# Matrix shapes, TensorE's order and the placing of side work in a graph layer followed by masked attention

## The chip, the cores and the metric

The kernel runs on one core of a Trainium2 chip. TensorE (PE in the profile) multiplies matrices into PSUM, VectorE (DVE), ScalarE (ACT) and GpSimd (POOL) work on SBUF, the first two also on PSUM, and all DMAs of this kernel are issued from SyncE's queue (SP). The metric is the device time of one launch in microseconds (us); lower is better. All data are float32, except for the mask, which is held as bytes.

## The reference

x is (8, 2048, 256), adj is (2048, 2048), sparse with a full diagonal. Two layers follow each other, both with a residual and a layernorm:

```python
# layer 0
A_norm = A + eye(n)
deg = A_norm.sum(0) + A_norm.sum(1) - diagonal(A_norm)
A_hat = A_norm * rsqrt(deg)[:, None] * rsqrt(deg)[None, :]
agg = einsum('nm,bmd->bnd', A_hat, x)
h = relu(batchnorm(agg.reshape(-1, d) @ W1.T + b1))     # 256 -> 512
x = layernorm(x + batchnorm(h @ W2.T + b2))             # 512 -> 256
# layer 1: 4 heads of 64
q, k, v = split(x @ W)
scores = einsum('bhid,bhjd->bhij', q, k) / 8 + where(adj == 0, -inf, 0)
x = layernorm(x + einsum('bhij,bhjd->bhid', softmax(scores), v))
```

## The kernel before

**Layer 0.** The adjacency is transposed on PE and kept in SBUF. For each of the 8 batch entries and each chunk of 512 nodes (32 chunks) PE aggregates (L209) and multiplies by W1 (L235); the hidden rows go to DRAM as h_d, and DVE writes the mask, one byte for an element, to mask_d in 16 pieces. Once the statistics of the first batchnorm are complete, a second loop (L280 to L304) loads h again, applies batchnorm and ReLU on ACT (L287), multiplies by W2 (L295), adds the bias and takes statistics on DVE and stores y_d. In its iteration i == 4, SP's queue also gets the load of the projection weights wq and of the whole mask (16 x 2048 bytes in each of 128 partitions).

**Layer 1, `attention`.** The work is cut into 64 units: batch entry b, head pair hp (two heads of 64 columns) and a chunk k of 512 queries, in that order of nesting. A unit has eight steps of two key tiles each (GJ = 2, key tile = 128 keys). All units and steps are numbered through, step g = unit * 8 + step. In each step

- `scores` computes, key tile by key tile, keys by queries for both heads into a PSUM tile ps_s of two banks; here each of the four 64 x 64 quarters of the array takes one head and one half of the 128 keys (L449). DVE subtracts the mask from it into an SBUF tile pt (L459), ACT takes the exponential (L465; a factor of 2^40 makes a masked element zero), and POOL adds the pt tiles up in two halves for the sum of the softmax (L470, L472);
- `weigh`, two steps behind (LAG = 2), multiplies pt with V into ps_o; the four quarters are two heads by two halves of the keys (L484), so that ps_o has two banks, whose halves `finish_copy` adds (ACT L494, DVE L495).

Side work hangs on the steps: `project` makes one of q, k, v for a chunk of 512 rows (L414, L423, copied by ACT); `prep_load`, `prep_bn`, `prep_res`, `prep_norm` and `prep_t` load a chunk of y and x of the next batch entry, apply the second batchnorm, turn y by PE transposes (L379), add the residual, layernorm, store x1 and turn it for the projections (L397); for a unit that has ended, `finish_sums` sums acc over the partitions (L505), and `finish` turns sums and output (L516, L527), divides and adds the residual; `emit`, in units of the second head pair, does the last layernorm and stores the rows. A layernorm is a chain DVE, POOL (the power of -1/2, L345), DVE, ACT.

A step has two slots for side work: slot 0 between scores and weigh, slot 1 after weigh. The 24 projections of a batch entry are spread one to a step. The PSUM pools are ps_s with 2 tiles of two banks, ps_o with 1 tile of two banks and ps_m with 2 tiles of one bank, which projections, transposes and sums share. All four chunks of the first batch entry are prepared in the written order before the first scores; the order in which an engine runs its instructions is otherwise set by the framework, which lists for each engine what it takes to be ready, earlier written first.

Of the kernel before, what the change touches and what calls it, by code (L numbers as in the profile page):

```python
# [28 lines left out]
def tile_gcn_then_masked_attention(  # L29
# [64 lines left out]
    with ExitStack() as kept:  # L94
# [182 lines left out]
        with tc.tile_pool(name="l0b", bufs=3) as lp, tc.tile_pool(  # L277
            name="psy", bufs=4, space=PSUM
        ) as psy:
            for i in range(NALL):  # L280
                h = hp_.tile([P, NH, CH], F32, name="h")
                nc.sync.dma_start(h, h_d[i])
                if i == 4:
                    nc.sync.dma_start(wq, wqkv.rearrange("(c p) f -> p c f", p=P))
                    nc.sync.dma_start(mask, mask_d)
                for f in range(NH):
                    nc.scalar.activation(  # L287
                        h[:, f, :], h[:, f, :], AF.Relu,
                        bias=sh1[:, f : f + 1], scale=sc1[:, f : f + 1],
                    )  # L290
                y = lp.tile([P, NO, CH], F32, name="y")
                for o in range(NO):
                    py = psy.tile([P, CH], F32, name="py")
                    for f in range(NH):
                        nc.tensor.matmul(  # L295
                            py,
                            w2s[:, f, o * P : (o + 1) * P],
                            h[:, f, :],
                            start=(f == 0),
                            stop=(f == NH - 1),  # L300
                        )
                    nc.vector.tensor_scalar(y[:, o, :], py, b2s[:, o : o + 1], None, op0=ALU.add)
                    nc.vector.bn_stats(st2[:, o, i, :], y[:, o, :])
                nc.sync.dma_start(y_d[i], y)  # L304
# [5 lines left out]
def attention(tc, x, out, adj, mask, wq, ident, ones, mhalf, sc2, sh2, sall, y_d, x1_d):  # L310
# [16 lines left out]
    with ExitStack() as ctx:  # L327
        ap_ = ctx.enter_context(tc.tile_pool(name="attn", bufs=2))
        ps_s = ctx.enter_context(tc.tile_pool(name="ps_s", bufs=2, space=PSUM))
        ps_o = ctx.enter_context(tc.tile_pool(name="ps_o", bufs=1, space=PSUM))  # L330
# [27 lines left out]
        def prep_load(b, k):  # L358
            yt[b, k] = ap_.tile([P, NO, CH], F32, name="yt")
# [77 lines left out]
        def scores(u, g):  # L437
# [4 lines left out]
            for j in range(g * GJ, (g + 1) * GJ):  # L442
                ps = ps_s.tile([P, 2, CH], F32, name="ps_s")

                for q in range(2):
                    for h in range(2):
                        hs = slice(h * HD, (h + 1) * HD)
                        c0 = j * P + q * HD
                        nc.tensor.matmul(  # L449
                            ps[q * HD : (q + 1) * HD, h, :],  # L450
                            kt[hs, c0 : c0 + HD],
                            qt[hs, k * CH : (k + 1) * CH],
                            start=True,
                            stop=True,
                        )
                pss.append(ps)
# [17 lines left out]
        def weigh(u, g):  # L474
            b, hp, _ = units[u]
            if g == 0:
                outs[u] = ps_o.tile([P, 2, CH], F32, name="ps_o")
            for j in range(g * GJ, (g + 1) * GJ):
                pt = probs.pop((u, j))

                for h in range(2):
                    for q in range(2):
                        qs = slice(q * HD, (q + 1) * HD)
                        nc.tensor.matmul(  # L484
                            outs[u][h * HD : (h + 1) * HD, q, :],
                            qkv[b, hp][2][qs, j, h * HD : (h + 1) * HD],
                            pt[qs, h, :],
                            start=(j == 0),
                            stop=(j == NT - 1),
                        )  # L490

        def finish_copy(u):
            ot = ap_.tile([P, CH], F32, name="ot")
            nc.scalar.copy(ot, outs[u][:, 0, :])  # L494
            nc.vector.tensor_add(ot, outs[u][:, 1, :], ot)  # L495
# [44 lines left out]

        per_b = HP * NCH * NG
        side = {}

        def at_step(g, s, f, *args):
            side.setdefault((g, s), []).append((f, args))

        def prep_at(b, k, g):
            at_step(g - 6, 0, prep_load, b, k)
            at_step(g - 2, 1, prep_bn, b, k)
            at_step(g, 0, prep_res, b, k, 0)  # L550
            at_step(g, 1, prep_res, b, k, 1)
            at_step(g, 1, prep_norm, b, k)
            for d in range(ND):
                at_step(g + 4, d, prep_t, b, k, d)

        for b in range(B):
            g0 = b * per_b
            for c in range(NCH):
                for w in range(3):
                    at_step(g0 + 3 + 3 * c + w, 1, project, b, 1, c, w)  # L560
            if b + 1 < B:
                for k, g in enumerate((17, 23, 29, 48)):
                    prep_at(b + 1, k, g0 + g)
                for c, g in enumerate((35, 41, 47, 54)):
                    for w in range(3):
                        at_step(g0 + g + 2 * w, 1, project, b + 1, 0, c, w)
        for u in range(len(units)):
            g0 = (u + 1) * NG
            at_step(g0 + 1, 1, finish_copy, u)
            at_step(g0 + 4, 0, finish_sums, u)  # L570
            at_step(g0 + 5, 0, finish, u)
            at_step(g0 + 5, 1, emit, u)

        for k in range(NCH):
            prep_load(0, k)
# [3 lines left out]
            prep_norm(0, k)  # L579
            for d in range(ND):  # L580
                prep_t(0, k, d)
            for w in range(3):
                project(0, 0, k, w)

        total = len(units) * NG
        LAG = 2
        for g in range(total + NG):
            if g < total:
                scores(*divmod(g, NG))
            for f, args in side.get((g, 0), ()):  # L590
                f(*args)
            if 0 <= g - LAG < total:
                weigh(*divmod(g - LAG, NG))
            for f, args in side.get((g, 1), ()):
# [210 lines left out]
```

## Time and profile before

| | |
|---|---|
| time, median of 3 runs | 4069.35 us (4067.44 to 4070.09) |
| profiled execution: its time | 4070.09 us |
| profiled execution: span | 4068.3 us |
| granted TensorE clock, mean | 0.979 |
| last matmul of the second loop of layer 0 (L295) ends | about 1415 us |
| first scores (L449) | 1443.3 us |
| DVE L459, mask subtraction | x1024, 1219 ns each |
| ACT L465, exponential | x1024, 1055 ns each |
| POOL L472 and L470, sums | x768 and x128, 2365 ns each |
| PE L414 (q, k) and L423 (v) | 256.1 and 130.9 us busy |
| PE L505 (sums) | 69.2 us busy |
| PE L379, L397, L516, L527 (transposes) | 42.7, 45.1, 41.7, 39.6 us busy |

A float32 matmul is shown as two instructions (two passes). The form "64*64" in a row is the part of the array that one instruction uses, rows by columns. Matmuls are pipelined, so a row's mean duration (606 ns for L449) is longer than the distance from one wave to the next, and the time that a group takes is read from start to start.

### The profile page before, as it was taken

Reading aid. Unit: us, or ns where it says so; the run is one execution under the profiler, and the core shown is the slowest. Engines: PE = TensorE matmul, PEld = TensorE weight load, DVE = VectorE, ACT = ScalarE, POOL = GpSimd, SP = SyncE. Lnnn points to the kernel's source line nnn. Section 1 sums busy time; section 2 is a strip of 40 time slices with the busy share of each in tenths; the row PEclk is TensorE's granted clock in tenths of the full one; section 3 lists DMA queues with packets and bytes.
Section 4 is the critical chain, followed back from the end, with each engine's and each line's share of the span. In section 5 each row is a group of like instructions: output and inputs, shape, how many; then the busy total and the mean of one; then the engine's idle time right before and its main releaser. Section 6 shows DMA issues by size and latency. Waiting matters only on the chain. (4 is left out here: it accounts for less than half of the span.)

```text
span 4068.3 us, 54545 instructions
## 1 busy us (share of the span) xinstructions
PE 3855.4 (95%) x22818; PEld 1544.6 (38%) x22818; DVE 1883.5 (46%) x2589; ACT 1667.1 (41%) x2077; POOL 2288.4 (56%) x1083
## 2 busy tenths in 40 slices
PE   7999999999989989999999999999999999999986
PEld 5444444444434433333333333333333333333322
DVE  5211111111124435666665665665656666566565
ACT  5000000000024345555555555555555555555544
POOL 0011101110100038888878987988888888888897
PEclk8999999999999989999999999999999999999998
DMA  5111101110146620000010000000000000000000
GB/s 215 65 47 52 52 27 46 52 52 31 47 158 219 208 80 22 22 32 27 17 42 22 22 32 22 32 32 22 32 22 32 27 27 27 27 17 17 6 6 17
DMA packets 94491, 198.34 MB, mean 49 GB/s; under 512 B 7072, under 2 KB 73120, under 8 KB 83872
## 3 DMA queue, kind: packets, MB, share of 16 engines
q1 hardware_dynamic: 94240, 194.80, 13.8%
q8 instruction: 181, 2.97, 0.3%
q14 instruction: 70, 0.57, 0.0%
HBM read 106.70 MB, written 88.08 MB: 48 GB/s over the span
## 5 line engine op out<-in xcount | busy, mean ns | idle before, releaser
L472 POOL TENSOR_TENSOR acc<-acc,pt 128x1024 f32<-128x1024 f32 x768 | 1816.2, 2365 | 320.8 <-ACT pt L465 272.9
L459 DVE TENSOR_TENSOR pt<-ps_s,mask 128x1024 f32<-128x1024 f32 x1024 | 1208.6, 1219 | 791.7 <-PE ps_s L449 765.2
L465 ACT ACTIVATE pt<-pt 128x1024 f32<-128x1024 f32 x1024 | 1069.4, 1055 | 769.7 <-DVE pt L459 743.5
L449 PE MATMUL ps_s<-qt,kt 64*64 64x512 f32 x8192 | 1021.8, 606 | 81.2 <-DVE pt L459 79.5
L484 PE MATMUL ps_o<-pt,v 64*64 64x512 f32 x8192 | 1009.6, 600 | 41.4 <-DVE ot L495 41.4
L209 PE MATMUL pa<-at,xb 128*128 128x512 f32 x2048 | 886.9, 593 | 0.0
L187 POOL TENSOR_SCALAR xb<-xb,dinv 128x256 f32<-128x256 f32 x112 | 103.0, 943 | 865.3 <-DMA xb<-in_x_dram 853.3
L209 PEld LDWEIGHTS pa<-at,xb 128*128 128x128 f32 x2048 | 389.5, 190 | 488.1 <-issue 483.0
L449 PEld LDWEIGHTS ps_s<-qt,kt 64*64 64x64 f32 x8192 | 287.1, 134 | 655.4 <-issue 427.9
L484 PEld LDWEIGHTS ps_o<-pt,v 64*64 64x64 f32 x8192 | 299.5, 134 | 613.3 <-issue 506.8
L242 ACT ACTIVATE h<-ph,b1s 128x512 f32<-128x512 f32 x128 | 87.9, 687 | 993.9 <-PE ph L235 993.9
L228 DVE TENSOR_TENSOR ag<-pa,dbc 128x512 f32<-128x512 f32 x64 | 44.3, 692 | 771.2 <-PE pa L209 771.2
L470 POOL TENSOR_TENSOR acc<-pt 128x1024 f32<-128x1024 f32 x128 | 302.9, 2366 | 83.3 <-ACT pt L465 83.3
L414 PE MATMUL pm<-x1t,wq 128*128 128x512 f32 x512 | 256.1, 625 | 0.5 <-ACT x1t L398 0.5
L295 PE MATMUL py<-h,w2s 128*128 128x512 f32 x512 | 224.7, 602 | 13.7 <-ACT h L287 13.7
L235 PE MATMUL ph<-ag,w1s 128*128 128x512 f32 x512 | 225.1, 592 | 0.0
L350 ACT ACTIVATE x<-x,ln_nm,ln_rs 128x256 f32<-128x256 f32 x256 | 134.1, 589 | 208.7 <-DVE ln_nm L346 208.7
L88 POOL TENSOR_TENSOR rs<-rs,mhalf 128x4 f32<-128x4 f32 (+1 forms) x2 | 1.7, 870 | 379.9 <-DVE rs L87 379.9
L243 DVE BATCH_NORM_STATS2 st<-h 128x6 f32<-128x512 f32 x128 | 88.9, 694 | 148.5 <-ACT h L242 148.5
L295 PEld LDWEIGHTS py<-h,w2s 128*128 128x128 f32 x512 | 98.8, 194 | 139.5 <-issue 116.5
L414 PEld LDWEIGHTS pm<-x1t,wq 128*128 128x128 f32 x512 | 88.4, 192 | 166.5 <-issue 125.2
L287 ACT ACTIVATE h<-h,sh,sc 128x512 f32<-128x512 f32 x128 | 93.3, 801 | 132.5 <-DMA h<-h_d 122.9
(79 smaller groups left out, 1800.7 us busy)
## 6 DMA issues: line engine op xcount, KB each, us to landing
h_d<-h SPq DMA_DIRECT2D x32, 1024.0 KB, 3.9
h<-h_d SPq DMA_DIRECT2D x32, 1024.0 KB, 5.9
a<-in_adj_dram SPq DMA_DIRECT2D x16, 1024.0 KB, 8.3
xb<-in_x_dram SPq DMA_DIRECT2D x32, 512.0 KB, 3.9
y_d<-y SPq DMA_DIRECT2D x32, 512.0 KB, 6.3
yt<-y_d SPq DMA_DIRECT2D x32, 512.0 KB, 3.3
x<-in_x_dram SPq DMA_DIRECT2D x32, 512.0 KB, 3.8
x_d<-x SPq DMA_DIRECT2D x32, 512.0 KB, 2.8
```

Source lines behind the costliest of these rows:

```text
L187: nc.gpsimd.tensor_scalar(t4[:, j, :], t4[:, j, :], dv, None, op0=ALU.mult)
L209: nc.tensor.matmul(pa, xs[b][m // TPC][:, m % TPC, d * P : (d + 1) * P], at[:, m, c * CH : (c + 1) * CH], start=(m == 0), stop=(m == NT - 1),)
L235: nc.tensor.matmul(ph, w1s[:, d, f * P : (f + 1) * P], ag[:, d, :], start=(d == 0), stop=(d == ND - 1),)
L295: nc.tensor.matmul(py, w2s[:, f, o * P : (o + 1) * P], h[:, f, :], start=(f == 0), stop=(f == NH - 1),)
L350: nc.scalar.activation(t[:, i, :], t[:, i, :], AF.Identity, bias=nm[:, i : i + 1], scale=rs[:, i : i + 1],)
L414: nc.tensor.matmul(pm, wq[:, d, wcols], xt[:, d, cols], start=(d == 0), stop=(d == ND - 1))
L449: nc.tensor.matmul(ps[q * HD : (q + 1) * HD, h, :], kt[hs, c0 : c0 + HD], qt[hs, k * CH : (k + 1) * CH], start=True, stop=True,)
L459: nc.vector.tensor_tensor(pt, pss[j - g * GJ], mask[:, j, None, k * CH : (k + 1) * CH].to_broadcast([P, 2, CH]), op=ALU.subtract,)
L465: nc.scalar.activation(pt, pt, AF.Exp, scale=2.0**MASK_EXP)
L470: nc.gpsimd.tensor_add(accs[u, q], probs[u, j - 1], pt)
L472: nc.gpsimd.tensor_add(accs[u, q], accs[u, q], pt)
L484: nc.tensor.matmul(outs[u][h * HD : (h + 1) * HD, q, :], qkv[b, hp][2][qs, j, h * HD : (h + 1) * HD], pt[qs, h, :], start=(j == 0), stop=( ...
```

## The change

The mask and wq: wq is loaded in iteration 2, and each of 16 iterations loads one sixteenth of the mask. In `attention` the order of TensorE's instructions is taken as written. Scores use 64 rows and 128 columns for a head (two matmuls for a key tile instead of four), the product with V 128 rows and 64 columns (again two instead of four); ps_o becomes one bank, twice, and `finish_copy` is a single ACT copy. yt gets three buffers. The steps have one slot for side work, after weigh; projections come at steps 2, 2 and 5 of each unit, prep_t at step 2, prep_res and prep_norm at step 5 of the unit before, in the units of the second head pair, one chunk to a unit. Only chunk 0 of the first entry is prepared wholly before the first scores; the rows of chunk 1 too; the rest hangs on the steps of the first unit.

```diff
--- before.py
+++ after.py
@@ -280,9 +280,10 @@
             for i in range(NALL):
                 h = hp_.tile([P, NH, CH], F32, name="h")
                 nc.sync.dma_start(h, h_d[i])
-                if i == 4:
+                if i == 2:
                     nc.sync.dma_start(wq, wqkv.rearrange("(c p) f -> p c f", p=P))
-                    nc.sync.dma_start(mask, mask_d)
+                if 4 <= i < 4 + NT:
+                    nc.sync.dma_start(mask[:, i - 4, :], mask_d[:, i - 4, :])
                 for f in range(NH):
                     nc.scalar.activation(
                         h[:, f, :], h[:, f, :], AF.Relu,
@@ -325,9 +326,11 @@
     GJ = 2
     NG = NT // GJ
     with ExitStack() as ctx:
+
+        ctx.enter_context(tc.manual_schedule(engines={mybir.EngineType.PE}))
         ap_ = ctx.enter_context(tc.tile_pool(name="attn", bufs=2))
         ps_s = ctx.enter_context(tc.tile_pool(name="ps_s", bufs=2, space=PSUM))
-        ps_o = ctx.enter_context(tc.tile_pool(name="ps_o", bufs=1, space=PSUM))
+        ps_o = ctx.enter_context(tc.tile_pool(name="ps_o", bufs=2, space=PSUM))
         ps_m = ctx.enter_context(tc.tile_pool(name="ps_m", bufs=2, space=PSUM))
 
         x1, x1t, yt, qkv = {}, {}, {}, {}
@@ -356,7 +359,7 @@
             return src[b, k * CH : (k + 1) * CH, :].rearrange("(t p) d -> p t d", p=P)
 
         def prep_load(b, k):
-            yt[b, k] = ap_.tile([P, NO, CH], F32, name="yt")
+            yt[b, k] = ap_.tile([P, NO, CH], F32, name="yt", bufs=3)
             nc.sync.dma_start(yt[b, k], y_d[b * NCH + k])
             x1[b, k] = ap_.tile([P, TPC, D], F32, name="x1", bufs=7)
             nc.sync.dma_start(x1[b, k], rows(b, k, x))
@@ -441,18 +444,12 @@
             pss = []
             for j in range(g * GJ, (g + 1) * GJ):
                 ps = ps_s.tile([P, 2, CH], F32, name="ps_s")
-
-                for q in range(2):
-                    for h in range(2):
-                        hs = slice(h * HD, (h + 1) * HD)
-                        c0 = j * P + q * HD
-                        nc.tensor.matmul(
-                            ps[q * HD : (q + 1) * HD, h, :],
-                            kt[hs, c0 : c0 + HD],
-                            qt[hs, k * CH : (k + 1) * CH],
-                            start=True,
-                            stop=True,
-                        )
+                for h in range(2):
+                    hs = slice(h * HD, (h + 1) * HD)
+                    nc.tensor.matmul(
+                        ps[:, h, :], kt[hs, j * P : (j + 1) * P], qt[hs, k * CH : (k + 1) * CH],
+                        start=True, stop=True,
+                    )
                 pss.append(ps)
             for j in range(g * GJ, (g + 1) * GJ):
                 pt = ap_.tile([P, 2, CH], F32, name="pt", bufs=10)
@@ -474,25 +471,21 @@
         def weigh(u, g):
             b, hp, _ = units[u]
             if g == 0:
-                outs[u] = ps_o.tile([P, 2, CH], F32, name="ps_o")
+                outs[u] = ps_o.tile([P, CH], F32, name="ps_o")
             for j in range(g * GJ, (g + 1) * GJ):
                 pt = probs.pop((u, j))
-
                 for h in range(2):
-                    for q in range(2):
-                        qs = slice(q * HD, (q + 1) * HD)
-                        nc.tensor.matmul(
-                            outs[u][h * HD : (h + 1) * HD, q, :],
-                            qkv[b, hp][2][qs, j, h * HD : (h + 1) * HD],
-                            pt[qs, h, :],
-                            start=(j == 0),
-                            stop=(j == NT - 1),
-                        )
+                    nc.tensor.matmul(
+                        outs[u][h * HD : (h + 1) * HD, :],
+                        qkv[b, hp][2][:, j, h * HD : (h + 1) * HD],
+                        pt[:, h, :],
+                        start=(j == 0),
+                        stop=(j == NT - 1),
+                    )
 
         def finish_copy(u):
             ot = ap_.tile([P, CH], F32, name="ot")
-            nc.scalar.copy(ot, outs[u][:, 0, :])
-            nc.vector.tensor_add(ot, outs[u][:, 1, :], ot)
+            nc.scalar.copy(ot, outs[u])
             outs[u] = ot
 
         def finish_sums(u):
@@ -538,60 +531,79 @@
                 nc.sync.dma_start(rows(b, k, out), t)
 
 
+
+        per_u = NG
         per_b = HP * NCH * NG
         side = {}
 
-        def at_step(g, s, f, *args):
-            side.setdefault((g, s), []).append((f, args))
-
-        def prep_at(b, k, g):
-            at_step(g - 6, 0, prep_load, b, k)
-            at_step(g - 2, 1, prep_bn, b, k)
-            at_step(g, 0, prep_res, b, k, 0)
-            at_step(g, 1, prep_res, b, k, 1)
-            at_step(g, 1, prep_norm, b, k)
+        def at_step(g, f, *args):
+            side.setdefault(g, []).append((f, args))
+
+        def prep_at(b, k, g, t):
+
+            at_step(g - 6, prep_load, b, k)
+            at_step(g - 2, prep_bn, b, k)
+            for half in range(2):
+                at_step(g, prep_res, b, k, half)
+            at_step(g, prep_norm, b, k)
             for d in range(ND):
-                at_step(g + 4, d, prep_t, b, k, d)
+                at_step(t, prep_t, b, k, d)
 
         for b in range(B):
             g0 = b * per_b
             for c in range(NCH):
-                for w in range(3):
-                    at_step(g0 + 3 + 3 * c + w, 1, project, b, 1, c, w)
-            if b + 1 < B:
-                for k, g in enumerate((17, 23, 29, 48)):
-                    prep_at(b + 1, k, g0 + g)
-                for c, g in enumerate((35, 41, 47, 54)):
-                    for w in range(3):
-                        at_step(g0 + g + 2 * w, 1, project, b + 1, 0, c, w)
+
+                u0 = g0 + c * per_u
+                if b or c:
+                    for w, g in enumerate((2, 2, 5)):
+                        at_step(u0 + g, project, b, 1, c, w)
+                if b + 1 < B:
+                    u0 = g0 + (NCH + c) * per_u
+                    prep_at(b + 1, c, u0 - 3, u0 + 2)
+                    for w, g in enumerate((2, 2, 5)):
+                        at_step(u0 + g, project, b + 1, 0, c, w)
         for u in range(len(units)):
             g0 = (u + 1) * NG
-            at_step(g0 + 1, 1, finish_copy, u)
-            at_step(g0 + 4, 0, finish_sums, u)
-            at_step(g0 + 5, 0, finish, u)
-            at_step(g0 + 5, 1, emit, u)
-
-        for k in range(NCH):
-            prep_load(0, k)
+            at_step(g0 + 1, finish_copy, u)
+            at_step(g0 + 4, finish_sums, u)
+            at_step(g0 + 5, finish, u)
+            at_step(g0 + 5, emit, u)
+
+
+        def first_rows(k):
             prep_bn(0, k)
             for half in range(2):
                 prep_res(0, k, half)
             prep_norm(0, k)
+
+        def first_columns(k):
             for d in range(ND):
                 prep_t(0, k, d)
             for w in range(3):
                 project(0, 0, k, w)
+
+        for k in range(3):
+            prep_load(0, k)
+        first_rows(0)
+        first_rows(1)
+        prep_load(0, 3)
+        first_columns(0)
+        at_step(0, first_rows, 2)
+        at_step(1, first_columns, 1)
+        at_step(2, first_rows, 3)
+        at_step(3, first_columns, 2)
+        at_step(5, first_columns, 3)
+        for w in range(3):
+            at_step(7, project, 0, 1, 0, w)
 
         total = len(units) * NG
         LAG = 2
         for g in range(total + NG):
             if g < total:
                 scores(*divmod(g, NG))
-            for f, args in side.get((g, 0), ()):
-                f(*args)
             if 0 <= g - LAG < total:
                 weigh(*divmod(g - LAG, NG))
-            for f, args in side.get((g, 1), ()):
+            for f, args in side.get(g, ()):
                 f(*args)
 
 
```

## Prediction

> **What bounds the kernel now.** I read the page's busy times first, then its costliest groups, the waits of PE over the steady part (1526 to 3739.6 us of the span), and last the timeline around single steps.
>
> ```profile
> PE 3855.4 (95%) x22818; PEld 1544.6 (38%) x22818; DVE 1883.5 (46%) x2589; ACT 1667.1 (41%) x2077; POOL 2288.4 (56%) x1083
> ...
> L449 PE MATMUL ps_s<-qt,kt 64*64 64x512 f32 x8192 | 1021.8, 606 | 81.2 <-DVE pt L459 79.5
> L484 PE MATMUL ps_o<-pt,v 64*64 64x512 f32 x8192 | 1009.6, 600 | 41.4 <-DVE ot L495 41.4
> ```
>
> PE is the bound: 95% busy, half of it in the two attention products. Its idle time in the steady part:
>
> ```profile
> PE ps_s L449 <- DVE pt L459: 53.0, 35, 3.1
> PE ps_o L484 <- DVE ot L495: 37.7, 27, 3.5
> ```
>
> First, scores wait for DVE to subtract the mask (L459) and so free a PSUM tile. Second, a unit's first product with V waits until the only ps_o tile is emptied (L494, L495). In the timeline I counted 128 L449 matmuls to a unit: unit 1 begins at 1526.1, unit 8 at 1806.7, unit 56 at 3739.6. One batch entry (8 units) takes (3739.6 - 1806.7)/6 = 322.2 us; units without projections in the last entry take 30.6.
>
> Now the price of a change of tile shape. First two steps with nothing between the products, then one with a projection (128*128):
>
> ```profile
> 1568.98 1.90 PE L484 MATMUL ps_o<-pt,v 64*64 64x512 f32 x16
> 1570.70 1.90 PE L449 MATMUL ps_s<-qt,kt 64*64 64x512 f32 x16
> 1572.42 1.90 PE L484 MATMUL ps_o<-pt,v 64*64 64x512 f32 x16
> ...
> 1507.61 1.98 PE L414 MATMUL pm<-x1t,wq 128*128 128x512 f32 x4
> 1509.52 1.95 PE L449 MATMUL ps_s<-qt,kt 64*64 64x512 f32 x16
> 1511.29 1.90 PE L484 MATMUL ps_o<-pt,v 64*64 64x512 f32 x16
> ```
>
> Start to start, 16 quarter-array matmuls take 1.72 us: four waves of four that run together, 0.43 a wave. With unchanged shape nothing is lost. L414's four waves take 1.91 (+0.19), the scores after it 1.77 (+0.05), and the V product before the next projection (at 1513.11) 1.82 (+0.10). A round trip costs 0.34 to 0.37, about 0.18 a switch.
>
> Last, what a layernorm on DVE does to PE:
>
> ```profile
> 2119.65 1.90 PE L484 MATMUL ps_o<-pt,v 64*64 64x512 f32 x16
> ...
> 2116.76 0.17 DVE L517 TENSOR_REDUCE sall<-pm 128x8 f32<-128x16 f32 x1
> ...
> 2120.55 1.64 DVE L344 TENSOR_SCALAR ln_rs<-ln_mv 128x4 f32<-128x4 f32 x1
> 2123.31 0.16 DVE L346 SCALAR_TENSOR_TENSOR ln_nm<-ln_mv,ln_rs 128x4 f32<-128x4 f32 x1 [1.13 <-POOL ln_rs L345]
> 2123.39 3.65 DVE L459 TENSOR_TENSOR pt<-ps_s,mask 128x1024 f32<-128x1024 f32 x3
> ```
>
> From 2116.76 to 2123.39 DVE does `finish` and a layernorm, 6.6 us without one mask subtraction; the next scores wait 3.12 us (start 2124.66).
>
> [...] L344, on 4 columns, takes 0.17 us alone and 1.64 above, while POOL accumulates.
>
> **The change part by part.**
>
> *Shapes.* Scores become K=64, 128 columns: 2 matmuls (of two passes) where there were 4. V becomes K=128, 64 columns. Both still fill the array with two tiles, so a group stays 1.72; 64*128 is in no row of the trace. I take it as concurrent like the row halves of 64*64. The two shapes differ, so every step now holds two switches: scores enter 0.11 and leave 0.10, V enters 0.05 and leaves 0.10, 0.36 a step. A step is 3.44 + 0.36 = 3.80; eight are 30.4. Whole-array work comes at steps 2 and 5 (+0.2 each for one more switch) and the sums (128*32) at step 4 (+0.13): 0.53. A unit is then 30.4 + 0.53 + sums 0.86 + finish transposes 0.86 = 32.65, with three projections of 1.72 each 37.8. Four prepared chunks an entry add 1.72 each: 8 x 37.8 + 6.9 = 309.3 us an entry without stalls. Before is 322.2, of which (53.0 + 37.7)/6.87 = 13.2 idle. [...]
>
> *ps_o twice, L495 dropped.* Removes the 37.7 (41.4 in all), included above. The ACT copy stays, beside PE.
>
> *Fixed order, and work gathered at steps 2 and 5.* Here I expect the loss. PE can no longer step past a wait, and ps_m has two tiles for everything.
> - Step 2 of the second four units: two prep_t transposes (0.43 each) fill both tiles, then q needs both ACT copies (L398 0.57 each) before it starts: 1.3 us, 4 times, 5.2.
> - Step 5 in written order: scores, V, v projection, prep_res twice, finish transposes. DVE then has, ahead of the next step's subtractions, two residual adds (0.68 each), a layernorm (1.75 of statistics, 1.64, 1.13 wait, 0.16 = 4.7), finish (1.9), and where the unit before was of the second head pair, another layernorm. PE can still do the next scores and V (1.83 + 1.87), then it needs a freed ps_s. With r the start of the first residual transpose: adds done r+2.1, layernorm r+6.8, finish r+8.7, second layernorm r+13.4, subtraction r+14.6. PE is out of work at r+6.5 (1.2 of it already waits for ps_m). With both layernorms that is a stall of 8 when DVE's order is as written; where finish and subtractions slip into the two waits for POOL (1.1 and 1.3; the trace does this in other places) 5.7. I take 6.5 for each of two units. One with a prepared chunk alone: r+9.9 less 6.5, minus what slips in: 3.0, twice. A final layernorm alone: 7.9 after the reduce against about 5 of PE work: 2.5, twice. Finish behind v alone: 0.4, twice, for the v copy. Sum 13 + 6 + 5 + 0.8 = 24.8.
>
> An entry becomes 309.3 + 5.2 + 24.8 = 339.3. Low end 315 (DVE subtracts first), high end 352 (as written, with slower clock after each stall; the trace's first scores after a 3.1 us stall took 2.04 instead of 1.72).
>
> *First unit.* Before, unit 0 takes 1443.3 to 1526.1, with 27 us of PE idle from 1416 and matmuls in half-filled waves. After: 8 scores and 6 V groups (14 x 1.72 = 24.1), three column preparations of 6.0, two row preparations 1.7, one projection set 5.2, 20 switches 3.6, and stalls of two layernorms (5 each) and three copies (1.3 each): 66.5, so unit 1 starts at 1510: -16 (bounds -27 to 0; before has two projections more behind it, which the unit costs above carry).
>
> *Mask in pieces.* One 4096 KB transfer stands ahead of h on SP; it ends in
>
> ```profile
> 1214.45 85.94 PE L295 MATMUL py<-h,w2s 128*128 128x512 f32 x195 [8.28 <-ACT h L287]
> ```
>
> Sixteen 256 KB pieces, each behind its h load and before a y store, add 16% to 1.5 MB per 6.9 us: -8 (bounds -8.3 to +5, if the pieces delay h). SP then also carries the earlier wq.
>
> *Last entry.* Four units at 37.8 plus one 2.5, then no projections: 32.65 against POOL's 14 x 2.365 = 33.1, so POOL binds: 33.3, then 37.9 twice as before's last full unit, then the same end (66.2): 331 against 328.7: +2.
>
> **Sum,** against the profiled execution (span 4068.3, its time 4070.1, 0.8 above the median 4069.35): steady part 7 x 339.3 - 40.3 (unit 0, counted above) = 2335 against 2213.5: +121; with -16, -8, +2: +99. Forecast 4170 us.
>
> **Rivals.**
> - *DVE's bursts stay covered.* Equal when an entry's stalls are 15 us, half of mine; below that the removed 13.2 idle wins. For it: before's preparations, next to a projection, cost 0.1 to 0.8. Against: the 3.12 above with less in one place. At 7 us: 4010.
> - *Switches dearer, or DVE wholly in written order.* 0.1 more a step is 512 x 0.1 = 51; 12 more an entry is 84: 4220 to 4300. For: 64*128 is unseen. Against: 64*64 loads of both row halves are hidden in one wave.
> - *Row halves do not run together.* Then scores double: 512 x 1.72 = 880, over 5000. Against: they do in 64*64.
> - *POOL as the bound* (33.1 of 38 to 47 us a unit) matters only at the end, as counted.
>
> **How the numbers follow.** Mine (4090 to 4220) 0.50; dearer 0.18; no concurrency 0.03; covered bursts 0.20 faster; the rest near the old time. A change within 0.2% (8 us) is what a measurement of this kernel cannot tell from none: 0.05. Faster 0.22, same 0.05, slower 0.73. Of the cases I leave out the fastest tenth and the dearest tenth: 4030 to 4280; the likeliest alone is 4090 to 4220.
>
> **What would show it.** Per step 3.80 start to start in steps 0, 1, 3; no L484 wait for ot; entries of about 339 with units 4 to 7 longer than 1 and 2 by 5 to 10 us; the wait of scores for DVE L459's successor grown from 53 to some 150 us, at steps 6 and 7; the 8.28 gone; unit 1 at about 1500. Wrong if a step costs other than 3.7 to 3.9, or if those waits stay near 50.

## The result, and the profile after

The changed kernel takes 4253.48 us (median of 4 runs, 4252.09 to 4254.68) against 4068.39 (4 runs, 4065.42 to 4070.09): a ratio of 1.0456, 95% interval 1.0438 to 1.0474. The profiled executions have spans of 4252.6 and 4068.3 us, 184.3 apart. All times below that are differences of stages come from these two.

The page's busy times and costliest groups, after (name, operation, out<-in, form, shape, count, then busy us, mean ns, idle us before, and what ended it):

```profile
PE 3969.5 (93%) x14626; PEld 1571.1 (37%) x14626; DVE 1862.0 (44%) x2525; ACT 1692.1 (40%) x2077; POOL 2283.6 (54%) x1083
...
L449 PE MATMUL ps_s<-qt,kt 64*128 64x512 f32 x4096 | 1072.7, 638 | 167.5 <-DVE pt L456 166.3
L478 PE MATMUL ps_o<-pt,v 128*64 128x512 f32 x4096 | 1015.9, 618 | 4.0 <-ACT pt L462 4.0
```

PE issues 8192 instructions fewer and is busy for longer. The wait for ot is gone, and the wait of scores for the mask subtraction (L459 before, L456 now) has doubled from 79.5 to 166.3 us. The busy time of the two groups themselves grew by 57.2 us, from 2031.4 to 2088.6.

Which waits of PE, in the steady part (units 1 to 55, from 1507.6 to 3914.4 us; who waited, for whom, us in total, times, longest):

```profile
PE ps_s L449 <- DVE pt L456: 150.4, 81, 6.9
PE pm L417 <- ACT x1t L401: 9.3, 28, 0.3
PE pm L520 <- ACT v L433: 8.1, 34, 0.2
PE pm L520 <- DVE x L384: 5.0, 21, 0.2
PE pm L382 <- ACT v L433: 5.0, 21, 0.2
PE pm L426 <- DVE x L384: 2.4, 7, 0.3
```

Together these are 180.2 us, against 92.5 before in the same units (53.0 for subtractions, 37.7 for ot, 1.8 other). The last five rows are the price of the fixed order with two ps_m tiles; it is 30 us.

The timeline of PE around one final layernorm and two steps after it (start, us, line, count, idle time before):

```profile
2856.14 2.33 PE L449 MATMUL ps_s<-qt,kt 64*128 64x512 f32 x8 [0.55 <-DVE pt L456]
2858.39 1.94 PE L478 MATMUL ps_o<-pt,v 128*64 128x512 f32 x8
2864.16 3.79 PE L449 MATMUL ps_s<-qt,kt 64*128 64x512 f32 x8 [3.83 <-DVE pt L456]
2867.88 2.94 PE L478 MATMUL ps_o<-pt,v 128*64 128x512 f32 x8
2870.74 1.99 PE L449 MATMUL ps_s<-qt,kt 64*128 64x512 f32 x8
2872.66 1.94 PE L478 MATMUL ps_o<-pt,v 128*64 128x512 f32 x8
2874.53 1.99 PE L449 MATMUL ps_s<-qt,kt 64*128 64x512 f32 x8
```

Read start to start, an undisturbed step is 2870.74 to 2874.53, 3.79 us: 1.92 for the scores, 1.87 for V. PE stands idle for 3.83 us, and then the scores take 3.72 and V 2.86 us, 2.8 more than usual. The view by stretches gives the reason, in its column for the granted clock (here 0.50, 0.64, 1.00; the columns before it are the busy times of PE, weight loads, DVE, ACT and POOL):

```profile
2864.10:2867.90 3.80, 3.74 (x10) 1.16 (x10) 2.36 (x3) 3.17 (x5) 1.73 (x1) 0.50 0.39 138
2867.90:2870.70 2.80, 2.80 (x10) 0.74 (x8) 1.23 (x1) 1.82 (x2) 2.72 (x2) 0.64 0.40 124
2870.70:2874.50 3.80, 3.80 (x18) 1.17 (x16) 2.35 (x2) 1.19 (x2) 2.63 (x3) 1.00 0.13 47
```

In the first stretch the clock is 0.50 throughout, and the scores take 1.94 times their usual 1.92 us. The 0.64 is a mean over a change: in the clock records of these two traces every value is 1.00 or 0.50, and the changes (79 in the kernel after, 51 before) lie whole multiples of 3.41 us apart.

The kernel before has such stretches too. Of its six waits of 3.12 us in units 1 to 55, the one that the prediction shows left the clock at 1.00: the scores from 2124.66 took 2.04 us instead of 1.72, and V was normal again. An equal wait in the same trace cost more:

```profile
1801.46 3.11 PE L449 MATMUL ps_s<-qt,kt 64*64 64x512 f32 x16 [3.12 <-DVE pt L459]
1804.35 2.51 PE L484 MATMUL ps_o<-pt,v 64*64 64x512 f32 x16
```

```profile
1802.20:1805.50 3.30, 3.30 (x20) 1.04 (x20) 2.42 (x3) 3.02 (x4) 2.03 (x1) 0.50 0.45 159
```

The scores took 2.89 us and V 2.33 (the next scores start at 1806.68), 1.8 us lost. Three of the six waits went this way; in the kernel after, all 27 waits of 3.8 us or more were followed by work at 0.50, within 0.9 us of their end. In units 1 to 55, and outside of its waits, PE had the clock of 0.50 for 114 us in the kernel after and for 44 in the kernel before. Half of it counts as lost, 57 us and 22, an estimate from the scores' 3.72 us at 0.50 against 1.92 at 1.00.

What DVE and POOL did in the stall of the kernel after (the scores from 2864.16), first DVE, then POOL:

```profile
2857.20 0.16 DVE L347 TENSOR_SCALAR ln_rs<-ln_mv 128x4 f32<-128x4 f32 x1
2860.68 2.30 DVE L349 SCALAR_TENSOR_TENSOR ln_nm<-ln_mv,ln_rs 128x4 f32<-128x4 f32 x1 [3.32 <-POOL ln_rs L348]
2862.90 1.21 DVE L456 TENSOR_TENSOR pt<-ps_s,mask 128x1024 f32<-128x1024 f32 x1
```

```profile
2857.32 2.35 POOL L469 TENSOR_TENSOR acc<-acc,pt 128x1024 f32<-128x1024 f32 x1 [4.18 <-ACT pt L462]
2859.62 1.02 POOL L348 TENSOR_TENSOR ln_rs<-ln_rs,mhalf 128x4 f32<-128x4 f32 x1
2860.61 2.34 POOL L469 TENSOR_TENSOR acc<-acc,pt 128x1024 f32<-128x1024 f32 x1
```

DVE is not at work here. It has asked POOL for the power of -1/2; POOL has just begun an accumulation of 2.35 us, then takes 1.02 for the power, and DVE stands at `ln_nm` for 3.32. Then this instruction on 128 x 4 elements takes 2.30 us, as long as the next accumulation beside it (2.34). The scores begun at 2856.14 end by about 2858.4, so their subtractions could have begun then; they are queued behind and begin at 2862.90. In units 1 to 55 of the kernel before, `ln_nm` never took more than 0.17 us and waited for POOL for 46.6 us in all, 2.3 at most; in the kernel after it took 2.30 us in 27 of its 55 executions, each time beside an accumulation on POOL, and 0.16 to 0.17 in the other 28, with no instruction on POOL beside it; it waited for 92.0 us, 4.6 at most.

By stage, from unit starts counted in the timeline: first scores at 1435.5 instead of 1443.3 (-7.8); unit 0 lasts 72.0 instead of 82.8 (-10.8); units 1 to 55 last 2406.8 instead of 2213.5 (+193.3); the rest 338.2 instead of 328.7 (+9.5). One batch entry: (3914.4 - 1811.5)/6 = 350.5 us, before 322.2.

### The profile page after: what moved, and what is told of

Read it like the earlier page. It is cut to its first block, busy times and chain, and to the rows that moved or that the text cites. A ratio compares the mean times of both kernels' runs of the same rounds, so it can differ in the third digit from the quotient of the medians.

```text
span 4252.6 us, 38138 instructions
## 1 busy us (share of the span) xinstructions
PE 3969.5 (93%) x14626; PEld 1571.1 (37%) x14626; DVE 1862.0 (44%) x2525; ACT 1692.1 (40%) x2077; POOL 2283.6 (54%) x1083
## 3 DMA queue, kind: packets, MB, share of 16 engines
q8 instruction: 117, 1.92, 0.2%
## 5 line engine op out<-in xcount | busy, mean ns | idle before, releaser
L456 DVE TENSOR_TENSOR pt<-ps_s,mask 128x1024 f32<-128x1024 f32 x1024 | 1210.3, 1217 | 959.4 <-PE ps_s L449 931.8
L449 PE MATMUL ps_s<-qt,kt 64*128 64x512 f32 x4096 | 1072.7, 638 | 167.5 <-DVE pt L456 166.3
L478 PE MATMUL ps_o<-pt,v 128*64 128x512 f32 x4096 | 1015.9, 618 | 4.0 <-ACT pt L462 4.0
L449 PEld LDWEIGHTS ps_s<-qt,kt 64*128 64x128 f32 x4096 | 356.5, 191 | 818.3 <-DVE pt L456 461.4
L478 PEld LDWEIGHTS ps_o<-pt,v 128*64 128x64 f32 x4096 | 253.3, 139 | 717.2 <-issue 603.7
L417 PE MATMUL pm<-x1t,wq 128*128 128x512 f32 x512 | 242.3, 617 | 19.7 <-ACT x1t L401 19.7
L417 PEld LDWEIGHTS pm<-x1t,wq 128*128 128x128 f32 x512 | 93.9, 193 | 148.8 <-issue 106.7
L235 PEld LDWEIGHTS ph<-ag,w1s 128*128 128x128 f32 x512 | 97.2, 190 | 122.7 <-issue 122.0
```

The costliest lines, as they stand in the source:

```text
L235: nc.tensor.matmul(ph, w1s[:, d, f * P : (f + 1) * P], ag[:, d, :], start=(d == 0), stop=(d == ND - 1),)
L417: nc.tensor.matmul(pm, wq[:, d, wcols], xt[:, d, cols], start=(d == 0), stop=(d == ND - 1))
L449: nc.tensor.matmul(ps[:, h, :], kt[hs, j * P : (j + 1) * P], qt[hs, k * CH : (k + 1) * CH], start=True, stop=True,)
L456: nc.vector.tensor_tensor(pt, pss[j - g * GJ], mask[:, j, None, k * CH : (k + 1) * CH].to_broadcast([P, 2, CH]), op=ALU.subtract,)
L478: nc.tensor.matmul(outs[u][h * HD : (h + 1) * HD, :], qkv[b, hp][2][:, j, h * HD : (h + 1) * HD], pt[:, h, :], start=(j == 0), stop=(j == ...
```

## The experiments

All are made from the changed kernel unless said. "Entry" is the mean of entries 1 to 6, "waits" those of scores for the subtraction over the whole span. Each is one run with its profile, except e12.

| run | time us | entry us | waits us | mean clock |
|---|---|---|---|---|
| before (profiled) | 4070.1 | 322.2 | 79.5 | 0.979 |
| after (profiled) | 4254.4 | 350.5 | 166.3 | 0.970 |
| e1 quarters again | 4186.1 | 341.3 | 167.2 | 0.969 |
| e2 before, new shapes alone | 4072.2 | 324.8 | 47.7 | 0.987 |
| e3 extra matmuls in the stalls | 4226.1 | 345.4 | 111.0 | 0.981 |
| e4 no power on POOL | 4069.9 | 327.6 | 48.0 | 0.988 |
| e5 TensorE's order free | 4236.7 | 348.4 | 114.3 | 0.977 |
| e6 rows prepared at step 0 | 4365.8 | 366.4 | 142.8 | 0.959 |
| e7 layernorm in two halves | 4187.8 | 341.3 | 116.7 | 0.977 |
| e8 e7, quarters, step 2 reordered | 4192.9 | 343.0 | 159.6 | 0.964 |
| e9 e7, DVE's order fixed | 4118.6 | 333.1 | 79.2 | 0.980 |
| e10 ln_nm on POOL | 4052.9 | 323.9 | 30.2 | 0.988 |
| e11 rebuilt | 3941.8 | 307.3 | 10.8 | 0.985 |
| e12 rebuilt, step 2 reordered | 3879.4 | 298.9 | 10.3 | 0.986 |

The kernel before took 4066.9 to 4072.0 beside these runs.

**The shapes, undone here and done alone there.** e1 puts both products on quarters again, with ps_o as before (the calls are shortened, and the same change of the product with V is not shown):

```diff
-                for h in range(2):
-                    nc.tensor.matmul(ps[:, h, :], kt[hs, j * P : (j + 1) * P], qt[hs, ...])
+                for q in range(2):
+                    for h in range(2):
+                        nc.tensor.matmul(ps[q * HD : (q + 1) * HD, h, :], kt[hs, c0 : c0 + HD], qt[hs, ...])
-            nc.scalar.copy(ot, outs[u])
+            nc.scalar.copy(ot, outs[u][:, 0, :])
+            nc.vector.tensor_add(ot, outs[u][:, 1, :], ot)
```

> The changed kernel with the shapes alone undone (both products on 64x64 quarters, ps_o of two banks once, finish_copy with its DVE add). Theory A (bursts on DVE at step 5, and the half clock after the long stalls they cause, make most of the loss; the two more shape switches a step cost only 0.36 us a step): a step without side work falls from 3.79 to 3.44 us, units 1 and 2 of an entry from 38.2 to 36 to 37, the long waits of scores for the mask subtraction stay (130 to 180 us in all), time 4100 to 4140. Rival B (the switches are the whole loss): at or below the kernel before, 4070 or less.

Units 1 and 2 of the first entry came to 36.7 us, the waits stayed (167.2), the time was 4186: 67 us of the 184 come back, 46 less than theory A hoped, since the waits for ot (35.1) and for the x1t copies (43.1 instead of 19.7) grew. The switches are a part of the loss and not the whole. e2 is the other half of this pair, the same edit the other way round on the kernel before.

> The kernel before with the shapes alone changed (64x128 and 128x64, ps_o of one bank twice, one ACT copy), its own slots and TensorE order kept. Theory A: 111 switches an entry become about 183, 72 x 0.18 = 13 us an entry or 90 in all, and the 41 us of waits for ot go: about 4120. Rival B (the switches are the whole loss): 4230 to 4260. If instead shapes are free: 4030.

4072.2: no change, and none of the three numbers. The switches are there (a unit of pure products and sums lasts 32.3 us instead of 30.6), but the waits for ot (41.4) and a third of those for subtractions (79.5 to 47.7) went, and the two sides came out even. Theory A had the switches right and the gains too small: in units 1 to 55 all waits of PE fell from 92 to 39 us and the cost of the low clock from 22 to 3, and these units still became 15 us longer. An estimate from these figures is that the shapes cost 87 us there, where 90 were expected. Why the waits for subtractions and the low clock went as well was not tested.

**The clock.** e3 adds, in the four places of an entry where the long stalls stand, two matmuls that nobody reads:

```diff
+        def warm(u):
+            b, hp, _ = units[u]
+            pm = ps_m.tile([P, CH], F32, name="pm")
+            for _ in range(2):
+                nc.tensor.matmul(pm, ones, qkv[b, hp][0][:, :CH], start=True, stop=True)
...
+            if g == 0 and u > 1 and u % 8 in (0, 1):
+                warm(u - 1)
             for j in range(g * GJ, (g + 1) * GJ):
+                if j == 1 and u % 8 in (6, 7):
+                    warm(u)
```

> The changed kernel with two more 128x128x512 matmuls, whose result nobody reads, at the place of each long stall (four places an entry, about 1.9 us each with its switches). Theory A (after a stall of 3.8 to 4.6 us the granted clock is 0.5 for some 5 us, which costs 11 to 14 us an entry on top of the idle time): the idle stretches are cut to under 3 us, the mean clock goes from 0.97 to 0.98 or more, and the time falls by 50 to 95 us to 4160 to 4200, though work was added. Rival (the loss is the idle time alone): no gain, 4250 to 4310.

The timeline of PE in e3, at a stall as above:

```profile
2844.46 1.94 PE L488 MATMUL ps_o<-pt,v 128*64 128x512 f32 x8
2846.33 1.98 PE L444 MATMUL pm<-qt,ones 128*128 128x512 f32 x4
2850.24 2.26 PE L459 MATMUL ps_s<-qt,kt 64*128 64x512 f32 x8 [1.93 <-DVE pt L466]
2852.43 1.94 PE L488 MATMUL ps_o<-pt,v 128*64 128x512 f32 x8
```

The added work (L444) fills the first half of the stall, 1.93 us of idle time are left, and the scores then take 2.19 us instead of 3.72. With added work the kernel became 27 us faster and the mean clock rose from 0.970 to 0.981. The direction is theory A's, the size half of what it expected. In units 1 to 55 the waits became 51 us shorter, of which the added matmuls took 46; the cost of the low clock fell from 57 us to 25, and the time by 31. No wait over 2.7 us is left there (the longest of the run, 5.5 us, is at the start of unit 62), and the clock fell all the same after 5 of the 13 waits of 1.9 us and after 8 of the 14 of 2.7. So some 30 us of the loss went when idle time was filled; the low clock was rarer then, not gone. What decides between waits of equal length was not shown.

**GpSimd's part in the layernorm.** e4 takes the power off POOL:

```diff
-            nc.gpsimd.tensor_tensor(rs, rs, mhalf[:, :TPC], op=ALU.pow)
+            nc.vector.reciprocal(rs, rs)
```

> The changed kernel with the power of -1/2 in the attention part's layernorms (GpSimd, L348) replaced by a reciprocal on VectorE: it leaves out the root, so that no layernorm goes through GpSimd. Theory A1 (what makes the bursts long is the round trip through GpSimd, whose queue holds an accumulation of 2.36 us ahead of the power, with VectorE's ln_nm waiting in order and the next mask subtractions behind it): waits of scores for the subtraction fall from 166 to under 70 us, no stall over 3 us, time 4060 to 4110. Rival C (it is the amount of VectorE work gathered in step 5): waits stay above 110 us, time 4190 to 4250.

PE's waits for subtractions in e4:

```profile
PE ps_s L449 <- DVE pt L456: 48.0, 51, 2.2
```

4069.9: the time is that of the kernel before again, with VectorE's work left as it was plus a reciprocal. e4 also tells the wait from the long instruction: in units 1 to 55 `ln_nm` still takes more than 0.3 us in 25 of its 55 executions, 2.1 at most. What carries the loss is therefore mainly the wait for the power, not the long instruction behind it. e10 keeps the power and takes away only VectorE's wait for it:

```diff
+            nc.vector.tensor_scalar(nm, mv[:, :, 0], -1.0, None, op0=ALU.mult)
             nc.gpsimd.tensor_tensor(rs, rs, mhalf[:, :TPC], op=ALU.pow)
-            nc.vector.scalar_tensor_tensor(nm, mv[:, :, 0], -1.0, rs, op0=ALU.mult, op1=ALU.mult)
+            nc.gpsimd.tensor_tensor(nm, nm, rs, op=ALU.mult)
```

> The changed kernel with the multiplication for ln_nm moved from VectorE to GpSimd, right behind the power (VectorE only negates the mean before it): VectorE asks GpSimd for nothing any more in a layernorm, ScalarE still waits for it. Theory A1: stalls over 3 us go, waits of scores under 90 us, 4070 to 4130. If ScalarE's wait in its place stops the exponentials and with them the product with V: little gain, 4180 to 4250, and PE waits on L462 appear.

4052.9, better than hoped. PE's waits in e10:

```profile
PE ps_s L448 <- DVE pt L455: 30.2, 31, 1.5
...
PE ps_o L477 <- ACT pt L461: 6.7, 2, 4.8
```

The feared wait behind ScalarE does not appear in units 1 to 55: both waits of the second row are in the last unit, where the kernel after has one of 4.0 us too. VectorE does the same statistics here, in the same step 5, no wait for a subtraction is over 1.5 us, and the granted clock is 1.00 throughout units 1 to 55. That settles the question between the wait for POOL and the amount of work gathered, as long as the framework may put subtractions between that work (e9 comes back to this). The changes of shape are still paid: these units last 2227.9 us, against 2213.5 before.

**The fixed order.** e5 drops the line with `manual_schedule`.

> The changed kernel with TensorE's order left to the framework again, all else as it is. Theory A (VectorE's order behind GpSimd's power makes the loss, which TensorE's order does not touch): the waits of scores for the subtraction stay above 110 us, the waits for ps_m's copies (some 35 us) shrink, time 4190 to 4270. Rival D (the fixed order is what costs): waits under 80 us, 4060 to 4120.

4236.7, 17 us less: the waits for ps_m's copies shrank (the x1t one from 19.7 to 4.4), and those for subtractions stayed above 110, though only just, at 114.3 instead of 166.3. Fixing TensorE's order is at most a small part of the loss. In units 1 to 55 all waits of PE fell by 80 us and the time by 12 only; PE goes from one part of the array to another 1266 times there instead of 1044, and how much of the gain this took up was not followed up.

**Where the work hangs.** e6 moves the preparation of rows (`prep_at(b + 1, c, u0 - 8, u0 + 2)` for `u0 - 3`).

> The changed kernel with the rows of the next entry's chunk (prep_res, prep_norm) moved from step 5 to step 0 of the same unit, so that no step has two layernorms. Theory C (the amount of VectorE work gathered in step 5): units 5 and 6 of an entry fall from 50 to 52 us to about 43, the stalls shrink to those of a lone layernorm, time 4110 to 4150. Theory A1 (each final layernorm waits for GpSimd by itself): the four stalls of an entry that follow a final layernorm stay at 3 us or more, units 5 and 6 fall to 46 to 48 only, time 4180 to 4210.

4365.8: both expectations missed, by far. PE's timeline in e6, at step 2 of unit 6:

```profile
2367.11 1.09 PE L400 MATMUL pm<-ident,x 128*128 128x128 f32 x8
2373.35 5.81 PE L417 MATMUL pm<-x1t,wq 128*128 128x512 f32 x8 [5.15 <-ACT x1t L401]
```

The projections wait 124.3 us in all for the copies of x1t, against 19.7 in the kernel after. ACT's timeline of the same moment:

```profile
2367.68 2.07 ACT L353 ACTIVATE x<-x,ln_nm,ln_rs 128x256 f32<-128x256 f32 x4 [2.36 <-DVE ln_nm L349]
...
2372.74 1.04 ACT L401 COPY x1t<-pm 128x512 f32<-128x512 f32 x2
```

The layernorm's scaling, which waits for ln_nm and so for POOL, now stands ahead of the copies on ScalarE. By these rows it is the same round trip, with another queue behind it. The eight projections take 5.74 us from start to start instead of 3.63 (2878.32 to 2881.95 in the kernel after), at a mean granted clock of 0.63: the low clock again.

**Moving the wait, and making it stay moved.** e7 cuts the layernorm at the power; the half that needs it is written two steps later:

```diff
-            layernorm(x1[b, k])
+            halves["p", b, k] = layernorm_a(x1[b, k])
...
+            at_step(g + 2, prep_norm_b, b, k)
...
+            at_step(g0 + 7, emit_b, u)
```

> The changed kernel with each layernorm of the steady part cut in two where GpSimd's power is asked for: the second half (ln_nm on VectorE, the scaling on ScalarE, the store) is written two steps later, behind the mask subtractions of those steps. Nothing is left out. Theory A1: the wait for the power is no longer ahead of subtractions, waits of scores under 80 us, mean clock 0.98 or more, time 4060 to 4110. Rival C (amount of VectorE work): 4200 or more, since the work in an entry is the same.

4187.8, between the two. In the trace the lone final layernorm is unchanged; DVE's timeline in e7:

```profile
2860.93 0.16 DVE L347 TENSOR_SCALAR ln_rs<-ln_mv 128x4 f32<-128x4 f32 x1
2864.42 2.30 DVE L352 SCALAR_TENSOR_TENSOR ln_nm<-ln_mv,ln_rs 128x4 f32<-128x4 f32 x1 [3.32 <-POOL ln_rs L348]
```

The framework drew ln_nm forward again, ahead of the subtractions that are written before it: it orders by when it takes an instruction to be ready. e9 fixes VectorE's order too (`engines={PE, DVE}`).

> e7 with VectorE's order fixed as written too, so that the second half of a layernorm cannot be drawn ahead of the mask subtractions of the two steps between. Theory A1 (VectorE standing at ln_nm for GpSimd's power, with subtractions queued behind it): the lone final layernorm's stall (3.8 us two steps later in the kernel after and in e7) goes, waits of scores fall under 90 us, mean clock 0.98 or more, time 4060 to 4120. Rival C (amount of VectorE work in step 5): 4170 or more.

4118.6, waits 79.2, longest 3.4: the edit works once the order holds. Units 0, 1 and 2 are 39.9, 38.2 and 38.2 us; units 5 and 6, with two layernorms in step 5, are still 45 to 47. So the amount of work gathered has a part after all, where two layernorms meet and VectorE's order is as written: before such a wait in e9, VectorE goes from 2690.47 to 2698.64, 8.2 us, through two residual adds, `finish` and the first halves of two layernorms without one subtraction, and without waiting for POOL. In e10, where its order is free, a subtraction is drawn in between (at 2665.29), and 1.5 us are left of that wait.

**A better version.** e8 was a first try to combine.

> e7 with both products on 64x64 quarters again (ps_o of two banks once) and, at step 2 of each unit, the side work written ahead of the product with V, to lie beside the emptying of ps_o. If the prices add up (0.36 us a step less, ot waits of 35 us mostly hidden): units 1 and 2 of an entry at about 36, an entry at 308 to 315, time 3940 to 3990. If VectorE or GpSimd binds first (33.1 us a unit for the sums): 4000 to 4040.

4192.9: units 1 and 2 of the first entry are 35.9, as hoped, but with VectorE's order free the waits are back (159.6), and at step 2 the projections, now ahead of V, wait 80.8 us for x1t. e11 takes up each cause (shortened below): quarters; order fixed on three engines; at step 5 transposes first, then the projections as work for PE while DVE normalises; all three projections of the next entry there, so that prep_t has no reader waiting; two layernorms never in one step.

```diff
-    engines={mybir.EngineType.PE}
+    engines={mybir.EngineType.PE, mybir.EngineType.DVE, mybir.EngineType.Activation}
-            at_step(g0 + 5, emit, u)
+            at_step(g0 + 6, emit, u)
+            at_step(g0 + 8, emit_b, u)
...
+                    for w in range(3):
+                        at_step(u0 + 5, project, b + 1, 0, c, w)
+                    at_step(u0 - 3, prep_norm, b + 1, c)
+                    at_step(u0 - 1, prep_norm_b, b + 1, c)
```

> A rebuilt version on what the runs showed: both products on 64x64 quarters; order fixed on TensorE, VectorE and ScalarE; at step 5 the transposes of rows and finish first, then the projections (all three of the next entry there, so that prep_t at step 2 has no reader waiting), then the first half of the preparing layernorm; the final layernorm's first half at step 6; second halves two steps later. If the prices add up (36.7 us a unit as in e1, stalls of scores under 40 us, clock 0.985): 3960 to 4010. If VectorE's fixed order costs PE more than it saves: 4070 or more.

3941.8. Its largest wait in the attention part is for ot, once a unit; e12 writes the side work of step 2 ahead of the product with V.

> e11 with the side work of step 2 (q and k projections, or prep_t) written ahead of the product with V, so that it lies beside the emptying of ps_o (61 us of waits in e11). If that wait is hidden in the units with projections at step 2 (36 of 64 units at 0.6 to 0.75 us) and partly in those with prep_t: 3900 to 3930, waits for ot under 35 us. If another wait takes its place (scores kept from ps_s, or the projections from ps_m): 3935 to 3960.

3879.35 us (median of 5 runs, 3878.22 to 3879.63) against 4068.37 beside it (9 runs), a ratio of 0.9536, interval 0.9523 to 0.9549; it beats both kernels. It also beats the expectation by 20 us. PE's waits in e12:

```profile
PE ps_o L493 <- DVE ot L504: 19.3, 18, 1.8
...
PE ps_s L458 <- DVE pt L468: 10.3, 32, 2.0
```

The ot waits fell from 60.9 to 19.3, which is 42 of the 62 us won. Another 5 are the low clock: units 1 to 55 of e11 have three stretches at 0.50, of 3.41 us each, those of e12 none. Where the rest comes from was not followed up. Each unit of the first entry, also 1 and 2, became 0.8 to 1.2 us shorter, more than the ot wait of most units, 0.5 to 0.8.

## Why the prediction came out as it did

Direction and order of the causes held, and 4253 us lies in the wide range, 4030 to 4280. It lies above the range called likeliest, 4090 to 4220, and among the numbers of the rival "switches dearer, or DVE wholly in written order" (4220 to 4300), for neither of its reasons: a step costs what was forecast, and two subtractions do slip in between a layernorm's instructions (at 2854.89 and 2856.09 in the kernel after). The gain of 8 us by the mask, the loss in the steady part and the place of it behind step 5's layernorms were forecast; the loss was 184 us, forecast were 100. Point by point:

- *Mask in pieces*, forecast -8: PE's wait of 8.28 us at this place is gone, and that was right. That the first scores come 7.8 us earlier is the sum of two things: the second loop of layer 0 ends 11.1 us earlier (1404.7 instead of 1415.8), and the way from there to the first scores, which the change also rebuilds, is 3.3 us longer.
- *First unit*, forecast 66.5 us with unit 1 at 1510 (1502 with the mask's 8 us): it lasted 72.0, unit 1 began at 1507.6. Right in kind, 5.5 too short.
- *Shapes and switches*, forecast 3.80 us a step: 3.79. 37.8 a unit without stalls: units 1 and 2 of the first entry lasted 38.2, with 0.24 of waiting. Row halves of 64*128 do run together: eight such instructions take 1.92 us, where four of 128*128 took 1.91 (L414). The cheapest-looking assumption, unseen in the trace of before, was right. The 0.05 to 0.11 for entering or leaving each of the new shapes were my estimate; the runs show only the sum, 3.79 us a step.
- *Waits for ps_m at step 2*, forecast 5.2 us an entry: 9.3/6.875 = 1.4 (6.875 is the number of entries in 55 units). Too high: PE could start q after 0.3 us at most.
- *Step 5's stalls*, forecast 24.8 us an entry: the waits for subtractions are 150.4/6.875 = 21.9, and 3.0 for ps_m. The sum was right by luck, for its parts were not: forecast were 6.5 us where two layernorms meet, 3.0 for a preparing one alone and 2.5 for a final one alone; in the entry from unit 24 on they are 5.5 to 6.0, 0.5 and 3.8. I had the longest stalls follow from the amount of DVE work with two layernorms in one step, and counted 1.1 to 1.6 us for each meeting with POOL. Measured at a lone layernorm were 3.32 us of waiting and 2.30 for ln_nm itself, and e10, which leaves the amount as it is, removes the stalls. The forecast that they would show at steps 6 and 7 was wrong too: small waits are there, the long ones come a step later, at step 0 of the next unit, because a step's subtractions do slip in ahead of ln_nm.
- *The terms that were missing.* An entry without stalls is 8 x 37.96 + 6.9 = 310.6 us, its waits are 180.2/6.875 = 26.2; together 336.8, against 350.5 measured and 339.3 forecast. Of the remaining 13.7 us an entry, 8.3 (57/6.875) are the low clock, which is in no term of my sum. I named a slower clock only for the high end, and read its price off one stall (0.3 us, at 2124.66) after which the clock had not fallen at all. Those 0.3 us are what a group of scores took longer at full clock after the waits seen: 2.04 us in the kernel before after 0.56 us of waiting as after 3.12, and in the kernel after 2.19 to 2.26 instead of 1.92, after 0.28 to 0.66. The wait at 1801.46, in the same trace, would have shown 1.8. The other 5.4 us an entry are not the clock: in e10 the clock is 1.00 in all of units 1 to 55, and an entry (323.9) still exceeds 310.6 and its waits (60/6.875 = 8.7) by 4.6. A part must be those 0.3 us, since PE waits 191 times in these units of the kernel after and 69 times before; it was not added up.
- *The steady part as a whole.* Units 1 to 55 became 193 us longer: 88 are waits of PE (180.2 less 92.5), 35 the low clock (57 less 22), and the other 70 the changes of shape and what waits cost beyond their length. e10 takes back 179 of them (2406.8 to 2227.9), nearly all by the first two.
- *Last entry*, forecast +2: +9.5. The terms of the forecast add up to 329, not 331. The four units with projections took 160.9 us instead of 153.7, and unit 56 alone 44.8: the wait of 3.83 us at its end and the low clock at its start belong to final layernorms, for which 2.5 were counted. The units behind them came out nearly as forecast, 177.3 against 175.3.

Of the rivals, covered bursts (4010) did not happen here, but e4 and e10 come close to it, 4070 and 4053. Dearer switches were not the reason, since a step costs 3.79. The shapes do cost time in both schedules: some 87 us in units 1 to 55 by e2's account, and some 106 by e1's, where these units are 63 us shorter although PE waits 43 us more and the low clock costs the same. In the old schedule other losses went at the same time, in the new one they stayed.

## What to carry to other kernels

When an engine in the middle of the main chain asks a slow engine for a tiny result, count the slow engine's whole instruction in progress (here 2.35 us of accumulation ahead of 1.02 for the power, 3.32 of waiting), and everything that is queued behind the asking one; move the second half of such an exchange behind the main chain's instructions, and check in the trace that it stayed there, since a framework that orders by readiness can draw it forward again (e7). Where PE is the bound, a stall's price is not its length alone: read the granted clock after it, and after several stalls of the kind, since equal ones differed here (0.3 and 1.8 us lost after 3.12). Removing the stalls brought the clock back whole here (e10, 1.00 in units 1 to 55); work hung there on purpose brought a part of it back (e3, a mean of 0.981 instead of 0.970).

## What the runs showed of the hardware that was not expected

- Equal waits of PE were followed by different clocks. After 3.12 us of idle time in the kernel before, the clock fell to 0.50 for 3.41 us in three cases of six (1.8 us lost at 1801.46) and stayed at 1.00 in the others (0.3 lost at 2124.66). It fell during or within 0.9 us after all 27 waits of 3.8 us or more in the kernel after, for 3.41 us or two or three times that, and in e3 after 5 of 13 waits of 1.9 us.
- In the kernel after, `ln_nm`, an instruction of DVE on 128 x 4 elements, took 0.16 us or 2.30, the latter beside a POOL accumulation of 2.34.
- Going from one part of the array to another and back cost about the same for the two pairs seen: 0.35 us a step for 64*128 and 128*64 (3.79 less two groups of 1.72, the time of a group of 64*64), 0.34 to 0.37 for 64*64 and 128*128. A weight load took 134 ns on average for 64*64 (before) and 139 for 128*64 (after, L478), 191 for 64*128 (L449) and 193 for 128*128 (L417), but 141 to 145 for 128*128 in the transposes of the attention part (L382, L400, L509, L520). What part of a change's cost it makes was not measured.
